# Moving five of seventeen first 3x3 convolutions of an image to VectorE, and two smaller edits

## The chip, the cores and the metric

The kernel runs on one core of a Trainium2 chip. It has a matrix engine (TensorE, PE in the profile; PEld is its loading of weights), a vector engine (VectorE, DVE), an activation engine (ScalarE, ACT), GpSimd (POOL) and SyncE (SP). Here the last two mostly issue DMA transfers. Results of TensorE land in PSUM, an accumulator memory, and another engine must copy them out ("evict" them). The metric is the device time of one execution in microseconds.

## The reference, cut to what matters

The input `x` is 8 images of 32 channels, 128 x 128, float32. All is float32 unless said. `CK = 32 * 8 = 256`.

```python
# layer 0, on g = group_norm(x)
# for each pixel: SSD over 3x3 patches with the 25 shifts of a 5x5 window, the 8 nearest,
# and those 8 shifted copies of g as 256 channels
xb = patch_match_stack(g)
dct = conv1x1(xb, dct_w, groups=C)
h = relu(conv3x3_depthwise(conv1x1(xb, w1), w2))       # "first" pair of convolutions
h = relu(conv3x3_depthwise(conv1x1(h, w3), w4))        # second
wiener = sigmoid(conv3x3_depthwise(conv1x1(h, w5), w6))  # third
x = x + conv1x1(conv1x1(wiener * dct, inv_dct_w, groups=C), agg_w)
# layer 1
x = x + conv5x5(group_norm(x), kernel, padding=2)
```

## The kernel before, in words

**Steps and slots.** Each image is worked in bands of R = 8 rows. There are 17 steps for an image (n = 0 to 16; the last, n = NS = 16, has no new rows and finishes those that the 3x3 convolutions still owe), and 136 for all eight, in one unbroken loop over s (line 917). Each step has four slots, i = 3, 2, 1, 0 in this order (line 928). Slot 1 does the first pair of convolutions (w1, w2) on the band of step s. Slot 2 does the second pair on the band of one step earlier, slot 3 the third on that of two steps earlier, and slot 0 the final part of that band: the product with the grouped 1x1 `dct_w` (`final_dct`, line 749), and in the next slot the sum over channels (`final_add`, line 762).

**Two halves of the channels.** The 256 channels are split. The upper 128 are always convolved by VectorE: `pointwise_v` (line 627) makes the 1x1 convolution with 128 x 128 products into the padded tile tv, ScalarE starts the accumulator (line 685), and VectorE adds the eight other taps with one instruction each (line 688). The lower 128 are convolved by TensorE: `pointwise_t` (line 647) makes the 1x1 convolution with 128 x 32 products into a tile t that has four row phases on the partitions, two transfers on SP (lines 670, 672) build the shifted copies, and `depthwise_t` (line 696) multiplies with small matrices of taps (line 709), which ScalarE evicts with the nonlinearity (line 721). `rows_before_t` and `rows_before_v` carry the two rows above a band over to the next step.

**The order of the work.** On TensorE, VectorE and ScalarE the program's order is the queue's order (ORDERED, line 15). SP and GpSimd are ordered by a planner. The loop writes the order out by hand with generators: a slot's TensorE convolution (dt) is issued in the next slot, in slot 0 ahead of the gather and elsewhere behind it; the last activation of VectorE's convolution (dv) comes at the end of the next slot.

**The gather.** While one band is convolved, the next is gathered: four units of work a step, one in each slot. `gather_load` (line 548) has GpSimd load a broadcast of indices into ib, five buffers; `gather_select` (line 578) makes ScalarE turn each ib into a 0/1 matrix sel with two instructions (lines 584, 585), for two halves, so four instructions a unit; `gather_pixels` (line 588) multiplies these with the shifted pixels on TensorE and has ScalarE evict them to xb (line 606). In slot order the load is three units ahead, the selection one, and both stand in the loop before `tick` and `pointwise_t`.

**Tasks.** The block matching of the next image, the normalisation and the 5x5 convolution of layer 1 are generators in queues D (VectorE), A (ScalarE), P and Q (TensorE). Each VectorE task has a cost in credits; `total` (line 883) is 183.8 for an image, and `tick` (line 886) lets tasks run as the credit owed grows: an image's total is spread over 14 steps (10 for the first image), two fifths of a step's share in slot 0 and a fifth in each other slot, and at most 6 credits stay owed.

Of the kernel before, what the change touches and what calls it, by code (L numbers as in the profile page):

```python
# [13 lines left out]
ALU = mybir.AluOpType  # L14
# [10 lines left out]
QW = TW + 4  # L25
HR = 38
HX = W + 4
SR = 6
EPS = 1e-5

# [13 lines left out]
def bm3d_conv_preact(  # L44
# [72 lines left out]
    tv = [const.tile([P, R + 2, W + 2], F32, name=f"tv{i}") for i in range(3)]  # L117
    for t in tv:
        nc.gpsimd.memset(t, 0.0)
    dwv = const.tile([P, 3, 9], F32, name="dwv")  # L120
    for n, w in enumerate((w2, w4, w6)):
        nc.sync.dma_start(dwv[:, n], w[P:CK].rearrange("p o a b -> p (o a b)"))
# [152 lines left out]
    def mixes():  # L275

        dq = work.tile([P, 2, K], F32, name="dq", tag="dq", bufs=1)
        for k in range(K):
            for m in range(2):
                nc.sync.dma_start(  # L280
                    dq[16 * k : 16 * (k + 1), m],
                    dct_w.rearrange("(m c i) k a b -> k m c (i a b)", m=2, i=K)[k, m],
                )
        m16 = work.tile([P, 16], F32, name="m16", tag="m16", bufs=1)
        yield "D", 1.0
        nc.vector.tensor_add(
            m16, cst[:, C_M32 : C_M32 + 16], cst[:, C_M32 + 16 : C_M32 + C]
        )
# [12 lines left out]
        for m in range(2):  # L301
            yield "D", 0.5
            ib = work.tile([P, P], F32, name=f"ib_{m}", tag="xm")
# [67 lines left out]
    def sources(b, xn):  # L371


        xl = dram.tile([H, W, C], F32, name=f"xl_{b}", tag="xl")
        for r in range(0, 32, 4):
            yield "P", 0
            pt = ps_x.tile([P, 4, P], F32, name=f"px_{b}_{r}", tag="x")
            for q in range(4):
                nc.tensor.transpose(pt[:, q], xn[:, 3 + r + q, 2 : 2 + W], ident)
            xs = work.tile([P, 4, P], F32, name=f"xs_{b}_{r}", tag="ct")  # L380
            nc.scalar.copy(xs, pt)
            for q in range(4):
# [68 lines left out]
    def costs(b, i, sq, idx):  # L451
# [35 lines left out]
        for h in range(0, R, 4):  # L487
# [6 lines left out]
            ct = work.tile([P, 4, P], F32, name=f"ct_{b}_{i}_{h}", tag="ct")  # L494
# [13 lines left out]
    def places(b, idx, i):  # L508
# [5 lines left out]
        o = work.tile([P, 256], F32, name=f"o_{b}_{i}", tag="lin_o", bufs=1)  # L514
        ct = work.tile([P, 256], F32, name=f"cn_{b}_{i}", tag="lin_c", bufs=1)
# [96 lines left out]
    def rows_before_t(i, b, n):  # L612

        t = tb[i - 1]
        if n < NS:
            nc.sync.dma_start(t[0:64, :, 0], t[64:P, :, 3])
        else:
            nc.gpsimd.memset(t[0:64, :, 0], 0.0)
# [8 lines left out]
    def pointwise_v(i, b, n, lhsT, src):  # L627
# [5 lines left out]
        for h in range(0, r1, 4):  # L633
# [10 lines left out]
            a = max(h, r0)  # L644
            nc.scalar.copy(v[:, 2 + a : 2 + h + hr, 1 : 1 + W], ps[:, a - h : hr])  # L645

    def pointwise_t(i, b, n, lhsT, src):
        t = tb[i - 1]
        nb = 2 if n < NS else 1
        if n == NS and i == 1:  # L650
            nc.gpsimd.memset(t[:, :, 2], 0.0)
        else:
            for q in range(2):
                ps = ps_x.tile([P, 2, 2, W], F32, name=f"p{i}_{b}_{n}_{q}", tag="x")
                for e in range(2):
                    s = slice(C * (2 * q + e), C * (2 * q + e + 1))
                    for g in range(2):
                        rows = src(g)
                        for r in range(4):
                            nc.tensor.matmul(  # L660
                                ps[C * r : C * (r + 1), e, :nb],
                                lhsT[:, g, s],
                                rows[:, r : r + 4 * nb - 3 : 4],
                                start=g == 0,
                                stop=g == 1,
                            )
                nc.scalar.copy(t[:, 2 * q : 2 * q + 2, 2 : 2 + nb], ps[:, :, :nb])  # L667
            for r in range(i - 1) if n == 0 else range(i - 1, 4) if n == NS else ():
                nc.gpsimd.memset(t[C * r : C * (r + 1), :, 2], 0.0)
        nc.sync.dma_start(t[64:P, :, 0:nb], t[0:64, :, 2 : 2 + nb])  # L670
# [2 lines left out]

    def depthwise_v(i, b, n):
        v = tv[i - 1]
        nr = R if n < NS else 4
        out_ = accp.tile([P, R, W], F32, name=f"acc{i}_{b}_{n}_1", tag=f"acc{i}1")
        acc = out_[:, :nr]
        for k, (dy, dx) in enumerate(
# [16 lines left out]
    def depthwise_t(i, b, n):  # L696
# [4 lines left out]
            ps_dw.tile([P, 2, 2, W], F32, name=f"pw{i}_{b}_{n}_{u}", tag=f"dw{u}")  # L701
            for u in range(2)
        ]
        for u in range(2):
            hi = 96 if u == 0 else P
            for dx in (0, -1, 1):
                xa, xz = max(0, -dx), min(W, W - dx)
                for j in range(4):
                    nc.tensor.matmul(  # L709
                        pt[u][C * j : C * (j + 1), :, :nb, xa:xz],  # L710
                        dwd[0:hi, i - 1, u, j, dx + 1],
                        t[0:hi, j, :, :nb, xa + dx : xz + dx],
                        start=dx == 0,
                        stop=True,
                        skip_group_check=True,
# [2 lines left out]
        acc = accp.tile([P, R, W], F32, name=f"acc{i}_{b}_{n}_0", tag=f"acc{i}0")  # L718
        rows = acc.rearrange("p (k e) w -> p e k w", e=4)
        for u in range(2):  # L720
            nc.scalar.activation(rows[:, u:4:2, :nb], pt[u][:, :, :nb], funcs[i - 1])  # L721
        rows_before_t(i, b, n)
        accs[i, b, n][0] = acc

# [64 lines left out]
    def layer1(b):  # L789
# [22 lines left out]
                nc.gpsimd.dma_start(xys[c], x1d[b][c : c + 4].rearrange("c y x -> y c x"))  # L812

        def normalise(c):
            xm = work.tile([P, 4, W], F32, name=f"xm_{b}_{c}", tag="xm")
            for i in range(4):
                nc.vector.tensor_scalar(
                    xm[:, i],
# [67 lines left out]
    def tick(b, i):  # L886

        now[0] += 1
        owed[0] += total / (NS - 2 if b else NS - 6) * (0.4 if i == 0 else 0.2)
        owed[0] -= run("D", owed[0]) if owed[0] > 0 else 0  # L890
        owed[0] = min(owed[0], 6.0)

# [8 lines left out]
    with tc.manual_schedule(engines=ORDERED):  # L901
# [8 lines left out]
            unit(gather_pixels, u - 3)  # L910
        u = 4

        dt = dv = kept = iter(())

        later = lambda: None

        for s in range(len(steps) + 2):
# [10 lines left out]
            for i in (3, 2, 1, 0):  # L928
# [6 lines left out]
                if live and i:  # L935
                    src = source(i, bi, ni)
                    pointwise_v(i, bi, ni, lws[i - 1], src)
                    new_v, new_t = depthwise_v(i, bi, ni), depthwise_t(i, bi, ni)
                    accs[i, bi, ni] = [None, next(new_v)]
                later()  # L940
                later = lambda: None
# [8 lines left out]

                run("Q")
                if s < len(steps):
                    unit(gather_select, u + 1)
                    unit(gather_load, u + 3)
                    tick(b, i)
                next(new_v, None)
                if live and i:
                    pointwise_t(i, bi, ni, lws[i - 1], src)
                next(kept, None)
                if not i:  # L960
                    next(dt, None)
# [78 lines left out]
```

## Time and profile before

| what | value |
|---|---|
| median of three runs | 7131.84 us (7118.07 to 7140.6) |
| the profiled execution | 7131.18 us, span 7129.4 us |
| mean granted TensorE clock | 0.978 |
| TensorE busy | 6700.9 us, 94% |
| VectorE busy | 5840.1 us, 82% |
| ScalarE busy | 5061.7 us, 71% |
| GpSimd busy | 2738.3 us, 38% |
| VectorE, taps of the upper half (line 688) | 3264 instructions, 4084.0 us, mean 1253 ns |
| TensorE, 3x3 of the lower half (line 709) | 19584 instructions, 2179.5 us |
| ScalarE, selections (lines 584 and 585) | 2048 instructions, 2249.8 us |

The profile is of one execution. "Busy" is the time in which an engine executes instructions; matmuls overlap each other, so the mean of one times the count is more than the busy time of their group. A row of the waits reads "engine, tile and line that waited <- what ended the wait: us in all, times, longest". A row of the timeline reads "start, length, engine, line, operation, out<-in, shapes, count", with the idle time just before it in brackets. The granted clock is the share of full speed that TensorE was allowed to run at.

### The profile page before, as it was taken

The numbers are of one execution on the slowest core, as the hardware profiler recorded it, in microseconds if no ns is written. First come the engines' busy times: TensorE is split into PE (matmuls) and PEld (weight loads), VectorE is DVE, ScalarE is ACT, GpSimd is POOL, SyncE is SP. The second block draws the span as 40 slices with busy tenths as digits, with TensorE's granted clock in tenths as the row PEclk, the third lists the DMA queues.
The fourth block names the chain that finished last, engine by engine and source line by source line (L and its number), as shares of the span: only waits on it lengthen the run. The fifth ranks groups of instructions, "written<-read, shape, count | busy, mean of one in ns | idle before, by whom it ended". The sixth has DMA issues, their size and how long they took to land. (4 is left out here: it accounts for less than half of the span.)

```text
span 7129.4 us, 229485 instructions
## 1 busy us (share of the span) xinstructions
PE 6700.9 (94%) x100226; PEld 3166.8 (44%) x100226; DVE 5840.1 (82%) x8606; ACT 5061.7 (71%) x6706; POOL 2738.3 (38%) x4599
## 2 busy tenths in 40 slices
PE   4699999999999999999999999999999999999997
PEld 1344444444444444444444444444444444444443
DVE  6689978888888898878888898888978889767675
ACT  4687768677686777867677776877768677666762
POOL 6244336333353343533335343543335333232222
PEclk8899999999999999999999999999999999999999
DMA  3566756666565575666656666566656666555652
GB/s 81 130 145 151 155 129 153 142 148 149 134 156 143 138 166 125 160 145 145 154 127 160 141 152 140 142 161 150 152 130 150 151 145 147 125 146 139 149 134 63
DMA packets 765484, 1007.70 MB, mean 141 GB/s; under 512 B 215008, under 2 KB 578592, under 8 KB 764480
## 3 DMA queue, kind: packets, MB, share of 16 engines
q0 software_dynamic: 378400, 733.67, 42.5%
q1 hardware_dynamic: 381056, 256.86, 17.0%
q8 instruction: 788, 12.91, 0.8%
q10 hardware_dynamic: 5024, 2.49, 0.2%
q14 instruction: 216, 1.77, 0.1%
HBM read 542.24 MB, written 217.01 MB: 106 GB/s over the span
## 5 line engine op out<-in xcount | busy, mean ns | idle before, releaser
L688 DVE SCALAR_TENSOR_TENSOR acc<-tv,dwv,acc 128x1024 f32<-128x1024 f32 (+1 forms) x3264 | 4084.0, 1253 | 223.1 <-ACT acc L685 109.5
L709 PE MATMUL pw<-t,dwd 128*32 128x508 f32 (+6 forms) x19584 | 2179.5, 592 | 156.8 <-DMA t<-t 109.4
L709 PEld LDWEIGHTS pw<-t,dwd 128*32 128x32 f32 (+1 forms) x19584 | 702.3, 111 | 1393.8 <-issue 1205.9
L570 POOL DMA_DIRECT2D ib<-idxd x1024 | 575.2, 563 | 1881.5 <-ACT sel L585 1764.8
L584 ACT ACTIVATE ib<-ib,nplace 128x1024 bf16<-128x1024 bf16 x1024 | 1165.4, 1138 | 25.6 <-DMA ib<-idxd 25.6
L585 ACT ACTIVATE sel<-ib 128x1024 f32<-128x1024 bf16 x1024 | 1084.4, 1059 | 32.6
L660 PE MATMUL p<-acc,lw 128*32 128x256 f32 x17408 | 994.1, 375 | 10.3 <-issue 10.0
L637 PE MATMUL pv<-acc,lw 128*128 128x512 f32 (+1 forms) x2112 | 971.9, 602 | 10.5 <-DVE acc L760 6.3
L606 ACT COPY xb<-pg 128x512 f32<-128x512 f32 x512 | 303.6, 593 | 713.5 <-PE pg L599 713.1
L645 ACT COPY tv<-pv 128x512 f32<-128x512 f32 (+2 forms) x784 | 444.8, 584 | 482.0 <-PE pv L637 463.6
L660 PEld LDWEIGHTS p<-acc,lw 128*32 128x32 f32 x17408 | 562.8, 110 | 429.6 <-issue 81.0
L721 ACT ACTIVATE acc<-pw 128x512 f32<-128x512 f32 (+1 forms) x816 | 452.8, 584 | 341.2 <-PE pw L709 340.8
L599 PEld LDWEIGHTS pg<-sel,xt 128*32 128x32 f32 x45056 | 591.2, 111 | 225.7 <-issue 126.1
L599 PE MATMUL pg<-sel,xt 128*32 128x48 f32 x45056 | 593.6, 206 | 82.9 <-issue 53.1
L780 DVE TENSOR_TENSOR xr<-xr,pa 128x256 f32<-128x256 f32 (+2 forms) x136 | 55.1, 405 | 717.9 <-PE pa L773 698.8
L637 PEld LDWEIGHTS pv<-acc,lw 128*128 128x128 f32 x2112 | 381.0, 191 | 407.7 <-issue 376.7
L410 DVE TENSOR_TENSOR df<-xn 128x786 f32<-128x786 f32 (+2 forms) x576 | 529.0, 969 | 17.2 <-PE pd L425 14.6
L667 ACT COPY t<-p 128x512 f32<-128x512 f32 x800 | 423.0, 570 | 119.8 <-PE p L660 116.5
L418 ACT ACTIVATE df<-df 128x786 f32<-128x786 f32 (+2 forms) x576 | 461.1, 862 | 50.4 <-DVE df L410 49.3
L685 ACT ACTIVATE acc<-tv,dwv 128x1024 f32<-128x1024 f32 (+1 forms) x408 | 459.8, 1127 | 45.8 <-PE pa L773 32.1
L637 PE MATMUL pv<-xb,lw 128*128 128x512 f32 x1024 | 475.7, 607 | 0.0
L757 PE MATMUL pc<-xf,ldct 128*128 128x512 f32 (+2 forms) x1056 | 470.9, 588 | 0.0
(128 smaller groups left out, 6397.3 us busy)
## 6 DMA issues: line engine op xcount, KB each, us to landing
ib<-idxd POOLq DMA_DIRECT2D x1024, 256.0 KB
xbd<-xb POOLq DMA_DIRECT2D x128, 1024.0 KB
xf<-xbd POOLq DMA_DIRECT2D x480, 256.0 KB
t<-t SPq DMA_DIRECT2D x792, 128.0 KB, 4.8
t<-t SPq DMA_DIRECT2D x384, 256.0 KB, 4.9
tv<-tv SPq DMA_DIRECT2D x384, 130.0 KB, 4.1
xt<-xtd POOLq DMA_DIRECT2D x240, 176.0 KB
xl<-xs POOLq DMA_DIRECT2D x256, 64.0 KB
```

What stands on the lines that cost most here:

```text
L410: nc.vector.tensor_sub(df[:, :, ca:cz], xn[:, r0 : r0 + SR, ca:cz], xn[:, r0 + dy : r0 + dy + SR, ca + dx : cz + dx],)
L418: nc.scalar.activation(df[:, :, ca:cz], df[:, :, ca:cz], AF.Square)
L570: nc.gpsimd.dma_start(ib.rearrange("p k y x -> p (k y x)"), idxd[b][s4 // 8, s4 % 8, 4 * k0 : 4 * k0 + 8] .rearrange("k x -> (k x)") .part ...
L584: nc.scalar.activation(ib, ib, AF.Square, bias=nplace)
L585: nc.scalar.activation(sel, ib, AF.Relu, scale=-1.0, bias=1.0)
L599: nc.tensor.matmul(pg[C * j : C * (j + 1), :, xa:xz], xt[:, t], sels[j // 2][:, j % 2, :, xa:xz], start=True, stop=True,)
L637: nc.tensor.matmul(ps[:, :hr], lhsT[:, g, P:CK], src(g)[:, h : h + hr], start=g == 0, stop=g == 1,)
L660: nc.tensor.matmul(ps[C * r : C * (r + 1), e, :nb], lhsT[:, g, s], rows[:, r : r + 4 * nb - 3 : 4], start=g == 0, stop=g == 1,)
L685: nc.scalar.activation(acc, rows, AF.Copy, scale=tap)
L688: nc.vector.scalar_tensor_tensor(acc, rows, tap, acc, op0=ALU.mult, op1=ALU.add)
L709: nc.tensor.matmul(pt[u][C * j : C * (j + 1), :, :nb, xa:xz], dwd[0:hi, i - 1, u, j, dx + 1], t[0:hi, j, :, :nb, xa + dx : xz + dx], start ...
L757: nc.tensor.matmul(ps[:, : z - a], ldct[:, m], xf[:, m, a:z], start=True, stop=True)
```

## The change

Three edits come together.

1. In steps n = 3, 5, 8, 10 and 13 of each image (DENSE), the first pair's lower 128 channels are convolved as the upper ones are. `pointwise_w` makes the 1x1 convolution with 128 x 128 products into a new padded tile tw, and `depthwise_w` has ScalarE start the accumulator, VectorE add eight taps, and ScalarE apply the ReLU. The eight taps are issued in slot 0 and the ReLU at the end of slot 3 (`old`). Since t and tw keep their rows in different layouts, eight transfers take two rows from t to tw before such a step (in `rows_before_t`) and eight take two rows from tw back to t in it. Tasks are charged 10.5 credits for each such step, and the image's total is raised by as much.
2. `gather_select` and `gather_load` move behind `gather_pixels` in the loop, so behind the evictions of `pointwise_t` and of the gather on ScalarE.
3. In the last step (n = 16) only the rows that count are made: `depthwise_v` makes i rows in place of 4, `depthwise_t` and `pointwise_t` leave out row phases that nobody reads.

To make room, the tiles xm, ib (of the setup), xs and ct share one tag with three buffers (before: two tags with two each), and the tiles o and cn of `places` lie in the buffer of v.

```diff
+DENSE = (3, 5, 8, 10, 13)
...
-            xs = work.tile([P, 4, P], F32, name=f"xs_{b}_{r}", tag="ct")
+            xs = work.tile([P, 4, P], F32, name=f"xs_{b}_{r}", tag="ct", bufs=3)
...
-        if n < NS:
+        if i == 1 and n + 1 in DENSE:
+            for q in range(4):
+                for r in range(2):
+                    nc.sync.dma_start(
+                        tw[C * q : C * (q + 1), r, 1 : 1 + W],
+                        t[C * (2 + r) : C * (3 + r), q, 3],
+                    )
+        elif n < NS:
             nc.sync.dma_start(t[0:64, :, 0], t[64:P, :, 3])
...
+    def pointwise_w(lhsT, src):
+
+        for h in range(0, R, 4):
+            ps = ps_x.tile([P, 4, W], F32, name=f"pvw_{h}", tag="x")
+            for g in range(2):
+                nc.tensor.matmul(
+                    ps, lhsT[:, g, 0:P], src(g)[:, h : h + 4], start=g == 0, stop=g == 1
+                )
+            nc.scalar.copy(tw[:, 2 + h : 6 + h, 1 : 1 + W], ps)
+        for q in range(4):
+            for r in range(2):
+                nc.sync.dma_start(
+                    tb[0][C * r : C * (r + 1), q, 0],
+                    tw[C * q : C * (q + 1), R + r, 1 : 1 + W],
+                )
+
+    def depthwise_w(b, n):
+        acc = accp.tile([P, R, W], F32, name=f"acc1_{b}_{n}_0", tag="acc10")
+        nc.scalar.activation(acc, tw[:, 1 : 1 + R, 1 : 1 + W], AF.Copy, scale=dww[:, 4:5])
+        yield
+        for k in (0, 1, 2, 3, 5, 6, 7, 8):
+            nc.vector.scalar_tensor_tensor(
+                acc,
+                tw[:, k // 3 : k // 3 + R, k % 3 : k % 3 + W],
+                dww[:, k : k + 1],
+                acc,
+                op0=ALU.mult,
+                op1=ALU.add,
+            )
+        yield
+        yield
+        nc.scalar.activation(acc, acc, funcs[0])
+        accs[1, b, n][0] = acc
...
+        nr = 4 if n < NS else i - 1
...
-                        for r in range(4):
+                        for r in range(nr):
...
-        nr = R if n < NS else 4
+        nr = R if n < NS else i
...
+        nh = [2 if n < NS else (i + 1 - u) // 2 for u in range(2)]
...
-                for j in range(4):
+                for j in range(4 if nh[u] else 0):
...
-        owed[0] += total / (NS - 2 if b else NS - 6) * (0.4 if i == 0 else 0.2)
+        owed[0] += (total + 10.5 * len(DENSE)) / (NS - 2 if b else NS - 6) * (0.4 if i == 0 else 0.2)
...
-                    new_v, new_t = depthwise_v(i, bi, ni), depthwise_t(i, bi, ni)
+                    dense = i == 1 and ni in DENSE
+                    new_v = depthwise_v(i, bi, ni)
+                    new_t = depthwise_w(bi, ni) if dense else depthwise_t(i, bi, ni)
...
-                    unit(gather_select, u + 1)
-                    unit(gather_load, u + 3)
                     tick(b, i)
                 next(new_v, None)
-                if live and i:
+                if live and i and dense:
+                    pointwise_w(lws[0], src)
+                    next(new_t)
+                    owed[0] -= 10.5
+                elif live and i:
                     pointwise_t(i, bi, ni, lws[i - 1], src)
                 next(kept, None)
                 if not i:
                     next(dt, None)
                 if s < len(steps):
                     unit(gather_pixels, u)
+                    unit(gather_select, u + 1)
+                    unit(gather_load, u + 3)
                     u += 1
                 if i:
                     next(dt, None)
                 run("A")
                 next(dv, None)
+                next(old, None)
                 next(dt, None)
-                kept, dv, dt = dv, new_v, new_t
+                kept, old, dv, dt = dv, dt, new_v, new_t
```

More of the change, by code (lines that the diff above doesn't have):

```diff
@@ L119, in bm3d_conv_preact @@
         nc.gpsimd.memset(t, 0.0)
+    tw = const.tile([P, R + 2, W + 2], F32, name="tw")
+    nc.gpsimd.memset(tw, 0.0)
+    dww = const.tile([P, 9], F32, name="dww")
+    nc.sync.dma_start(dww, w2[0:P].rearrange("p o a b -> p (o a b)"))
     dwv = const.tile([P, 3, 9], F32, name="dwv")
@@ L302, in mixes @@
             yield "D", 0.5
-            ib = work.tile([P, P], F32, name=f"ib_{m}", tag="xm")
+            ib = work.tile([P, P], F32, name=f"ib_{m}", tag="ct", bufs=3)
             nc.vector.tensor_tensor(
@@ L493, in costs @@
                 held.clear()
-            ct = work.tile([P, 4, P], F32, name=f"ct_{b}_{i}_{h}", tag="ct")
+            ct = work.tile([P, 4, P], F32, name=f"ct_{b}_{i}_{h}", tag="ct", bufs=3)
             nc.scalar.copy(ct[:, :, 0 : 4 * NO], pt[:, :, 0 : 4 * NO])
@@ L513, in places @@
         yield "D", 2.6
-        o = work.tile([P, 256], F32, name=f"o_{b}_{i}", tag="lin_o", bufs=1)
-        ct = work.tile([P, 256], F32, name=f"cn_{b}_{i}", tag="lin_c", bufs=1)
+        oc = work.tile([P, R, W + 2], F32, name=f"oc_{b}_{i}", tag="v", bufs=1)
+        oc = oc.rearrange("p r w -> p (r w)")
+        o, ct = oc[:, 0:256], oc[:, 256:512]
         nc.vector.tensor_copy(
@@ L666, in pointwise_t @@
                             )
-                nc.scalar.copy(t[:, 2 * q : 2 * q + 2, 2 : 2 + nb], ps[:, :, :nb])
+                nc.scalar.copy(
+                    t[: C * nr, 2 * q : 2 * q + 2, 2 : 2 + nb], ps[: C * nr, :, :nb]
+                )
             for r in range(i - 1) if n == 0 else range(i - 1, 4) if n == NS else ():
@@ L707, in depthwise_t @@
                 xa, xz = max(0, -dx), min(W, W - dx)
-                for j in range(4):
+                for j in range(4 if nh[u] else 0):
                     nc.tensor.matmul(
-                        pt[u][C * j : C * (j + 1), :, :nb, xa:xz],
+                        pt[u][C * j : C * (j + 1), : nh[u], :nb, xa:xz],
                         dwd[0:hi, i - 1, u, j, dx + 1],
-                        t[0:hi, j, :, :nb, xa + dx : xz + dx],
+                        t[0:hi, j, : nh[u], :nb, xa + dx : xz + dx],
                         start=dx == 0,
@@ L720, in depthwise_t @@
         for u in range(2):
-            nc.scalar.activation(rows[:, u:4:2, :nb], pt[u][:, :, :nb], funcs[i - 1])
+            if nh[u]:
+                nc.scalar.activation(
+                    rows[:, u : u + 2 * nh[u] - 1 : 2, :nb], pt[u][:, : nh[u], :nb], funcs[i - 1]
+                )
         rows_before_t(i, b, n)
@@ L814, in normalise @@
         def normalise(c):
-            xm = work.tile([P, 4, W], F32, name=f"xm_{b}_{c}", tag="xm")
+            xm = work.tile([P, 4, W], F32, name=f"xm_{b}_{c}", tag="ct", bufs=3)
             for i in range(4):
@@ L911, in bm3d_conv_preact @@
         u = 4
-        dt = dv = kept = iter(())
+        dt = dv = kept = old = iter(())
         later = lambda: None
```

## The prediction, made before the changed kernel was run

> **What bounds the kernel now.** I read the page's busy times first, then the windows of one image step by step, then the waits, then the order of time around one wait.
>
> ```profile
> PE 6700.9 (94%) x100226; PEld 3166.8 (44%) x100226; DVE 5840.1 (82%) x8606; ACT 5061.7 (71%) x6706; POOL 2738.3 (38%) x4599
> ```
>
> TensorE looks like the bound, with VectorE at 82%. An average hides the stages, so I cut image 4 into groups of steps. A window runs from the final product (line 757) of one step to that of the next. The columns are length, then the busy time of PE, PEld, DVE, ACT, POOL, clock, DMA.
>
> ```profile
> 3836.90:4059.00 222.10, 220.20 (x3098) 102.50 (x3095) 182.44 (x285) 157.18 (x202) 71.77 (x123) 1.00 0.63 145
> 4059.00:4352.80 293.80, 286.66 (x4509) 135.75 (x4508) 264.23 (x503) 218.79 (x290) 111.58 (x195) 0.99 0.67 154
> 4352.80:4483.80 131.00, 125.95 (x1787) 56.57 (x1785) 105.30 (x96) 83.34 (x109) 37.98 (x70) 1.00 0.55 128
> 4483.80:4683.10 199.30, 190.74 (x3144) 97.68 (x3140) 172.82 (x188) 169.14 (x235) 119.68 (x185) 0.99 0.64 156
> 6646.80:6879.80 233.00, 229.18 (x3685) 108.22 (x3681) 169.99 (x151) 172.69 (x220) 66.66 (x122) 1.00 0.64 148
> ```
>
> They are steps 3 to 6, 7 to 12, 13 to 15, then 16 with 0 to 2 of the next image; the last is five steps of the last image. TensorE has 2 us of idle time in steps 3 to 6 and VectorE 40. In steps 7 to 12 VectorE is busy 264 of 294 us, so only 30 us are left there. The last image has no block matching for a next one, and VectorE has 63 us left in five steps.
>
> ```profile
> PE pw L709 <- DMA t<-t: 109.4, 53, 12.1
> POOL ib L570 <- ACT sel L585: 1764.8, 468, 13.0
> ACT ib L584 <- DMA ib<-idxd: 25.6, 6, 10.0
> ...
> 3611.21 1.13 ACT L584 ACTIVATE ib<-ib,nplace 128x1024 bf16<-128x1024 bf16 x1
> 3612.38 1.06 ACT L585 ACTIVATE sel<-ib 128x1024 f32<-128x1024 bf16 x1
> 3613.34 1.05 ACT L667 COPY t<-p 128x512 f32<-128x512 f32 x2
> 3614.42 0.59 SPq L670 DMA_DIRECT2D t<-t  x1
> 3615.06 1.14 SPq L672 DMA_DIRECT2D t<-t  x1
> 3620.24 7.03 PE L709 MATMUL pw<-t,dwd 96*32 96x512 f32 x48 [2.30 <-DMA t<-t]
> ```
>
> The first line is TensorE's largest wait with a named cause; the last six show how it comes about. The product whose result t holds had ended at 3610.96, but ScalarE was in its four selection instructions and copied t out only at 3613.34. Its two transfers landed late, the convolution waited 2.30 us, and then took 7.03 us, where an undisturbed one takes 5.33.
>
> **The change, part by part.** All sums are against the profiled execution, 7131.2 us (span 7129.4 and 1.8 around it), which is 0.7 below the median: no correction.
>
> *Selections behind the evictions.* Nothing is added. From the first window (334 us) to the last image's end the trace has 48 waits for t<-t of together 88 us, and 18 of the products behind them are slow, together by 36 us (14 of them by 1.70 each). So at most 124 us can go. About two fifths of the waits lie in steps where VectorE has only 2 to 4 us of idle time (0, 9 to 12), which will bind next; I take 70. From the other side: between slot 0 and slot 3 the selections now stand ahead of the copies to tv. At 6659.26 ScalarE started such a copy; four selection instructions (1.138 + 1.059, twice) would put it some 3 to 4 us later and VectorE's convolution with it. What hides that is VectorE's tasks ahead of it, or its idle time (40 us in steps 3 to 6); with no cover in any step it would cost 3.5 x 136 = 476 us. I take 0. GpSimd's two loads a slot (0.56 us each) move with the selections, so their lead over the reader stays two slots; on its queue they now stand behind the store of xb, which waits 77 us in all for its eviction. ScalarE waits 25.6 us for the loads; twice that would cost 26 more. I take 0.
>
> The Trainium skill, "TensorE: Matmul & The Clock Gate", section "HAM oscillation", asks only that TensorE have no idle gap above about 3.4 us. The trace disagrees: 2.30 us was enough for the half rate, while at 5663.8 a gap of 1.57 left 5.33. By the rule the 36 us would not be there to win, and this part would be worth 50.
>
> *The convolution moved.* Per dense step (40 of them) TensorE loses 48 passes of line 709, 5.33 us, and 64 of line 660 (3.66) for 8 like line 637 (3.70): 213 us in all. VectorE gains 8 x 1.284 = 10.3 us, 411 in all. ScalarE gains line 685 and 692 (1.15 + 1.06) and loses two of line 721 (0.60 each): 1.0 us each, 41 in all, hidden at 71% busy. SP issues 8 transfers before the step and 8 in it, and four fewer of the old: 12 x 0.59 = 7.1 us per dense step. They read or fill rows that are used a step (50 us) later against 4.8 to land, so I take 0; should the planner put eight ahead of a t<-t transfer that is just in time, that convolution starts 4.7 us later, 40 x (4.7 + 1.7) = 256 us at the worst. The tiles that now share three buffers (xs, ct, xm) can make ScalarE wait for VectorE's searches; bounded by the present 62.6 us that VectorE waits for ct, taken as 0.
>
> What matters is when the new result is wanted. It is made in slot 0 and read by the first product of slot 2. From the end of line 757, TensorE has 1.09 (gather) + 1.07 (line 773) + 3.70 + 3.66 + 1.09 = 10.6 us of other work. VectorE needs 0.69 + 10.3 and ScalarE 1.06: 12.1, plus VectorE's backlog b. So TensorE will wait 1.5 + b. Behind the waiting activation on ScalarE stand only slot 2's evictions, since the next selections and the gather's eviction are ahead of it. The 5.33 saved is used up at b = 3.8, or at 2.1 if the wait halves the clock. The backlog can be read from when the four multiplications end against line 757's end. In step 5 VectorE stood waiting, in step 13 it was far behind:
>
> ```profile
> 3950.47 0.69 DVE L760 TENSOR_TENSOR acc<-acc,pc 128x512 f32<-128x512 f32 x1 [3.41 <-PE pc L757]
> 4352.35 10.52 DVE L688 SCALAR_TENSOR_TENSOR acc<-tv,dwv,acc 128x1024 f32<-128x1024 f32 x8
> 4362.78 2.48 DVE L760 TENSOR_TENSOR acc<-acc,pc 128x512 f32<-128x512 f32 x4
> ```
>
> In image 4, b is about 0.2 in step 3, 0 in 5, 2.8 in 8, 4.5 in 10, 8.1 in 13, and 1.4 in the last image. The gains are 3.6 and 3.8 in steps 3 and 5; steps 8, 10 and 13 come to +0.7, +2.4 and +6.0 lost. The 10.5 credits taken off hold tasks back in slots 0 and 3 and shrink these losses; I take 0, 1 and 3. That leaves 3.4 per image, 24 for seven, and 5 x (5.33 - 2.9) = 12 for the last: 36 us.
>
> *The pace of tasks.* Tasks go from 13.1 to 16.9 credits a step, less 10.5 in a dense one, so they still end with step 13. A credit is 0.90 us (5840 less 4084 in line 688, 322 in 760 and 105 in 780 and 781, over eight images: 166 us for 183.8). Steps without the extra work get 3.4 us more; steps 7, 9, 11 and 12 had 6.8, 3.9, 1.7 and 8.1 us of VectorE idle. I take a loss of 1.5 per image, 10 us.
>
> *The last step.* A convolution takes 48 passes in 2.79 us (0.058 each). At half the width a pass takes 0.030 (line 660: 64 in 1.95), so the three keep 24 x 0.030, 48 x 0.030 and 24 of each: 2.1 + 1.3 + 0.7 less, 32 us over eight images. VectorE's 24 instructions shrink from 0.751 to about 0.35, 0.43 and 0.59 (line 329 with 128 elements, line 522 with 256, and between for 384): 57 us, where it already idles 8 to 12 a step. I take 25.
>
> Sum: 7131 - 70 - 36 + 10 - 25 = **7010**.
>
> [...]
>
> **The rivals.**
>
> *TensorE stays the bound everywhere.* For it: it idles 2 us in steps 3 to 6, and the totals after would still be 6701 - 213 - 32 = 6456 against 5840 + 411 - 57 = 6194. Against: steps 7 to 12. All of it but the 1.5 us waits: 7131 - 213 + 60 - 32 - 124 = 6822.
>
> *VectorE becomes the bound: slower.* Place: the wait in slot 2. In steps 7 to 12 an undense window needs 34.4 + 15.2 = 49.6 us of VectorE against some 46.5 of TensorE. If that surplus is never drained, b is 2 in steps 3 and 5 and about 6, 8 and 11 in 8, 10 and 13; with the half clock these cost 3.9 + 5.9 + 8.9, less 3.6: 15 per image, 106 for seven. Selections then bring 30, the last step 25: 7182; with 3 us in each of four undense windows too, 7266. It decides above a mean b of 3.8; the five of image 4 have 3.1. For it: step 13's 8.1. Against: steps 3 and 5, and the credits.
>
> *The parts cancel.* The waits for t<-t turn into waits for a late tv, and the dense steps bring nothing: 7131 - 25 = 7106.
>
> **How the numbers follow.** A measurement of this kernel can tell about 0.3% (21 us) from no change; its runs span 7118 to 7141. Chances: my forecast 0.45 (6930 to 7085), TensorE the bound 0.17 (6790 to 6930), cancelling 0.14 (7085 to 7150), VectorE the bound 0.24 (7150 to 7270). Faster is the first two and 0.05 of the third, same 0.09, slower 0.24. Cutting about a tenth at each end gives 6850 to 7190.
>
> **What would show it.** Right: waits for t<-t well under half of 109; t copied straight after its product; VectorE near 6190 busy; the first product of slot 2 late by 1 to 3 us in steps 3 and 5 and by more in 8 to 13, behind ScalarE's last activation of the new accumulator; steps 3 to 6 shorter, 7 to 12 not. Wrong: steps 7 to 12 shorter by 10 us or more (b drained), or new waits of TensorE for selections, for transfers queued on SP, or for tv.

## The result: slower by 3.8%

The changed kernel takes 7404.5 us (median of four runs, 7391.9 to 7411.5) against 7136.2 for the kernel before. The ratio is 1.0378, 95% interval 1.0353 to 1.0403. The forecast was 7010, and 6850 to 7190 the range. The profiled execution has a span of 7409.4 us, 280 more than before. The medians and ratios below leave out two executions, of 10554.0 us (the kernel before) and 23234.3 us (the kernel with the third pair), whose granted clocks were 0.605 and 0.553.

The busy times of the changed kernel, from its page:

```profile
PE 6642.3 (90%) x95234; PEld 3105.2 (42%) x95234; DVE 6195.0 (84%) x8926; ACT 5118.6 (69%) x6698; POOL 2732.6 (37%) x4600
```

VectorE is at 6195 us, as worked out (6194), and ScalarE 57 us up (41 worked out). TensorE should have lost 244 us and lost 59: the passes that were taken out are gone (17472 of the 3x3 in place of 19584), and others became slower, with the mean granted clock at 0.954 in place of 0.978. Its idle time went from 428 to 767 us. So the time went into pauses of TensorE and into slow products around them.

The same groups of steps of image 4 (3 to 6, 7 to 12, 13 to 15, 16 with 0 to 2), changed kernel; length first, then busy PE, PEld, DVE, ACT, POOL, then clock, DMA share and GB/s:

```profile
4004.90:4231.80 226.90, 207.84 (x2919) 96.82 (x2915) 202.73 (x293) 154.75 (x196) 69.36 (x120) 0.96 0.55 135
4231.80:4554.90 323.10, 291.25 (x4250) 136.45 (x4246) 282.68 (x509) 226.10 (x294) 114.70 (x199) 0.95 0.61 138
4554.90:4690.00 135.10, 124.04 (x1741) 55.60 (x1737) 113.91 (x105) 84.40 (x109) 36.21 (x67) 0.96 0.51 124
4690.00:4910.60 220.60, 201.73 (x3010) 97.95 (x3007) 174.92 (x208) 174.09 (x241) 119.36 (x187) 0.98 0.60 144
```

All four groups became longer, by 5, 29, 4 and 21 us. In steps 7 to 12 VectorE had 30 us of idle time before and has 40 now, TensorE 7 before and 32 now. Neither is full: they wait.

What TensorE waits for in the changed kernel, from the waits:

```profile
PE pv L651 <- ACT acc L692: 240.1, 40, 8.9
PE pd L431 <- ACT df L424: 140.7, 89, 3.1
PE pi L541 <- DVE oc L532: 67.1, 12, 19.7
...
PE pw L762 <- DMA t<-t: 28.1, 10, 6.0
```

And the row of the squares in the kernel before:

```profile
PE pd L425 <- ACT df L418: 29.5, 29, 2.9
```

Line 651 is the 1x1 product of `pointwise_v`, line 692 the ReLU of the new dense convolution, lines 424 and 431 the squares of the block matching and the product that sums them. Before, the second wait was 29.5 us in 29 times, and the first had no counterpart. The wait for the indices of the block matching (lines 532 and 541) was 42.7 us before. The wait for t<-t, 109.4 us before, is down to 28.1.

The 40 waits for the ReLU are nearly all alike: 38 of them are between 5.89 and 5.97 us, whatever VectorE had to do. One of them, in the order of time, ScalarE and then TensorE and VectorE:

```profile
7034.82 0.59 ACT L613 COPY xb<-pg 128x512 f32<-128x512 f32 x1 [0.91 <-PE pg L606]
7035.30 1.15 ACT L591 ACTIVATE ib<-ib,nplace 128x1024 bf16<-128x1024 bf16 x1
7036.48 1.06 ACT L592 ACTIVATE sel<-ib 128x1024 f32<-128x1024 bf16 x1
7037.45 1.13 ACT L591 ACTIVATE ib<-ib,nplace 128x1024 bf16<-128x1024 bf16 x1
7038.61 1.06 ACT L592 ACTIVATE sel<-ib 128x1024 f32<-128x1024 bf16 x1
7039.58 1.04 ACT L692 ACTIVATE acc<-acc 128x1024 f32<-128x1024 f32 x1
...
7034.02 0.76 PE L606 MATMUL pg<-sel,xt 128*32 128x48 f32 x51 [0.34 <-issue]
7040.67 5.99 PE L651 MATMUL pv<-acc,lw 128*128 128x512 f32 x8 [5.89 <-ACT acc L692]
...
7029.33 7.89 DVE L682 SCALAR_TENSOR_TENSOR acc<-tw,dww,acc 128x1024 f32<-128x1024 f32 x6
7037.14 0.41 DVE L836 TENSOR_TENSOR xr<-xr,pa 128x256 f32<-128x256 f32 x1
```

VectorE's last tap ended at about 7037.1. ScalarE was then in the moved selections, which stand in its queue between the gather's eviction and the ReLU, and came to the ReLU at 7039.58 without having been idle since 7034.8. From the end of the gather to the end of the ReLU it is 0.59 + four selection instructions + 1.04, which is the 5.9. The product behind the pause then took 5.99 us, where it takes 3.70 at full clock; behind the 40 pauses it took between 5.11 and 6.71. Pause and slow product are 8.2 us, and the convolution that was saved is 5.33.

So the theory after the result: two parts of the change get in each other's way on ScalarE, and the moved selections also stand before the squares. The rival is the one of the prediction: VectorE is late with its extra taps.

### The profile page after: what moved, and what is told of

Read it like the earlier page. It is cut to its first block, busy times and chain, and to the rows that moved or that the text cites. A ratio compares the mean times of both kernels' runs of the same rounds, so it can differ in the third digit from the quotient of the medians.

```text
span 7409.4 us, 220482 instructions
## 1 busy us (share of the span) xinstructions
PE 6642.3 (90%) x95234; PEld 3105.2 (42%) x95234; DVE 6195.0 (84%) x8926; ACT 5118.6 (69%) x6698; POOL 2732.6 (37%) x4600
## 5 line engine op out<-in xcount | busy, mean ns | idle before, releaser
L739 DVE SCALAR_TENSOR_TENSOR acc<-tv,dwv,acc 128x1024 f32<-128x1024 f32 (+3 forms) x3264 | 4031.1, 1237 | 294.9 <-ACT acc L736 175.0
L762 PE MATMUL pw<-t,dwd 128*32 128x508 f32 (+6 forms) x17472 | 1923.8, 588 | 96.4 <-issue 43.9
L651 PE MATMUL pv<-acc,lw 128*128 128x512 f32 (+1 forms) x2112 | 1066.2, 651 | 278.2 <-ACT acc L692 240.1
L762 PEld LDWEIGHTS pw<-t,dwd 96*32 96x32 f32 (+1 forms) x17472 | 613.8, 111 | 1178.7 <-issue 1125.2
L709 PE MATMUL p<-acc,lw 128*32 128x256 f32 x16768 | 1027.0, 381 | 9.3 <-issue 5.3
L651 PEld LDWEIGHTS pv<-acc,lw 128*128 128x128 f32 x2112 | 415.6, 209 | 734.5 <-issue 425.6
L716 ACT COPY t<-p 128x512 f32<-128x512 f32 (+1 forms) x720 | 404.7, 578 | 425.3 <-PE p L709 414.1
L431 PE MATMUL pd<-df,neg 128*32 128x390 f32 (+2 forms) x2304 | 372.2, 531 | 146.0 <-ACT df L424 140.7
L775 ACT ACTIVATE acc<-pw 128x512 f32<-128x512 f32 (+1 forms) x728 | 381.2, 567 | 143.6 <-PE pw L762 143.6
L736 ACT ACTIVATE acc<-tv,dwv 128x1024 f32<-128x1024 f32 (+3 forms) x408 | 454.7, 1114 | 28.4 <-PE pa L829 14.9
```

Of the source, the lines that this page charges most:

```text
L651: nc.tensor.matmul(ps[:, :hr], lhsT[:, g, P:CK], src(g)[:, h : h + hr], start=g == 0, stop=g == 1,)
L709: nc.tensor.matmul(ps[C * r : C * (r + 1), e, :nb], lhsT[:, g, s], rows[:, r : r + 4 * nb - 3 : 4], start=g == 0, stop=g == 1,)
L736: nc.scalar.activation(acc, rows, AF.Copy, scale=tap)
L739: nc.vector.scalar_tensor_tensor(acc, rows, tap, acc, op0=ALU.mult, op1=ALU.add)
L762: nc.tensor.matmul(pt[u][C * j : C * (j + 1), : nh[u], :nb, xa:xz], dwd[0:hi, i - 1, u, j, dx + 1], t[0:hi, j, : nh[u], :nb, xa + dx : xz ...
```

## The experiments

Each is given by its edit against the changed kernel, unless another is named. Ratios are against the kernel before on the same chip. Where "..." stands, lines of a diff are left out.

### The ReLU ahead of the selections

```diff
                     unit(gather_pixels, u)
+                next(old, None)
+                if s < len(steps):
                     unit(gather_select, u + 1)
                     unit(gather_load, u + 3)
...
                 next(dv, None)
-                next(old, None)
```

> The changed kernel, with the last activation (ReLU) of the dense convolution issued before the four selection instructions of its slot instead of behind them. Theory A (ScalarE's order): the constant wait of 5.92 us at the first product of slot 2, 40 times, is the gather's eviction (0.59), four selection instructions (4.3) and the ReLU (1.04) behind the gather. Then the wait falls to what VectorE leaves, 3.4 us where its taps end 2.3 us after the gather, less elsewhere, and most of the slow products behind it (5.99 for 3.70) go: 40 x (2.5 to 4.8) = 100 to 190 us less, about 7215 to 7305. Theory B (VectorE's backlog, the prediction's rival): VectorE is what is late; the wait stays near 5.9 and the time near 7405.

Measured: 7289.8 us, ratio 1.0193 (1.0176 to 1.0210), by the ratios 1.85%, some 130 us, less than the changed kernel. Its waits:

```profile
PE pv L651 <- ACT acc L692: 110.5, 40, 5.3
PE pd L431 <- ACT df L424: 132.7, 87, 3.1
```

And, from the view of the ReLU's line, what ScalarE sat idle for before it (us, times); in the changed kernel this list is empty:

```profile
  DVE acc L682: 41.8, 21
```

The wait more than halved. Nineteen of the 40 are at 1.63 to 1.67 us, which is the gather's eviction and the ReLU alone; in the others ScalarE now does wait for VectorE. Both theories hold a part: the order was what bound, VectorE is next.

### Half of the taps

Four of the eight taps of the dense convolution are left out, so that result is incomplete.

```diff
-        for k in (0, 1, 2, 3, 5, 6, 7, 8):
+        for k in (0, 1, 2, 3):
```

> The changed kernel with four of the eight taps of the dense convolution left out (40 x 4 VectorE instructions, 206 us of VectorE; that result is not computed in full). Theory A (ScalarE's order): VectorE was not what TensorE waited for; the 40 waits stay at 5.9 us and the time within 60 us of 7405. Theory B (VectorE's backlog): the waits shrink by 5.1 us each and with them the slow products, 200 to 300 us less: 7100 to 7200.

Measured: 7405.4 us in a single execution, with 199 us less of busy VectorE.

```profile
PE pv L651 <- ACT acc L692: 240.0, 40, 8.9
```

The waits are what they were with all eight taps (240.1). Theory A holds, and the rival falls for the kernel as it was changed.

### Half of the taps, with the ReLU ahead

The same edit on the kernel with the ReLU ahead of the selections; again the result is incomplete.

> The kernel with the ReLU ahead of the selections (7290), with four of the eight taps of the dense convolution left out (206 us of VectorE; that result is not computed in full). Theory A: with the order mended VectorE is now late in half of the 40 waits (those above 1.65 us), so all 40 fall to 1.65, which is the gather's eviction and the ReLU, and the time falls by 40 to 110 us: 7180 to 7250. Rival: what is left of the loss has nothing to do with the taps but with the selections ahead of the squares; the waits above 1.65 stay or the time stays within 30 us of 7290.

Measured: 7202.8 us, ratio 1.0055 (1.0038 to 1.0072), by the ratios 1.4%, some 100 us, less than with all eight taps.

```profile
PE pv L651 <- ACT acc L692: 66.5, 40, 1.7
PE pd L431 <- ACT df L424: 139.5, 88, 3.1
```

All 40 waits are now 1.7 us or less. So with the order mended, VectorE's lateness is worth some 100 us; with the order as in the change it is worth nothing, since it was covered.

### The selections alone

The kernel before, with only the selections moved:

```diff
-                    unit(gather_select, u + 1)
-                    unit(gather_load, u + 3)
                     tick(b, i)
...
                     unit(gather_pixels, u)
+                    unit(gather_select, u + 1)
+                    unit(gather_load, u + 3)
```

> The kernel before with the selections and loads moved behind the gather and nothing else. Theory A (squares): the squares of the block matching now stand behind 4.3 us of selections on ScalarE, and TensorE's product of squares waits for them as in the changed kernel (118 us in all, against 8 before, and slow products behind); the waits for t<-t (109) go. Net 20 to 120 us slower: 7155 to 7255. Rival (the prediction): only the waits for t<-t go, 70 us faster, about 7065.

Measured: 7230.4 us, ratio 1.0115 (1.0098 to 1.0132).

```profile
PE pd L425 <- ACT df L418: 144.7, 104, 3.2
PE pw L709 <- DMA t<-t: 28.5, 19, 5.2
```

The waits for t<-t went from 109 to 28 us, as forecast. The wait for squares came, 115 us more than before, and the product of squares itself took longer (252.8 us of TensorE before, 299.1 now, each instruction counted up to the start of the next). Less 81, plus 115, plus 46 makes 80, near the 82 between the medians. The list is not complete: the two profiled executions differ by 92 us, the wait for the indices (line 534) rose from 42.7 to 72.1, and pauses before the gather for which the profile names no cause fell from 53.1 to 23.7. One place where squares are waited for, ScalarE and then TensorE:

```profile
2059.69 0.59 ACT L606 COPY xb<-pg 128x512 f32<-128x512 f32 x1 [5.49 <-PE pg L599]
...
2064.45 3.08 ACT L418 ACTIVATE df<-df 128x780 f32<-128x780 f32 x4
...
2065.34 2.76 PE L425 MATMUL pd<-df,neg 128*32 128x390 f32 x14 [1.11 <-ACT df L418]
```

ScalarE waited 5.49 us for the gather with no selection to do, then had the four selections before it, and the squares came 4.2 us after the eviction. TensorE waited 1.11 us for the first square and then went at ScalarE's pace, which made four squares in 3.08 us. The granted clock is 1.00 in this stretch and 0.980 in the whole run, so here TensorE is fed slowly and its clock is not cut. Where the selections stood before, they filled that idle time.

VectorE, too, waits more: for the accumulator that ScalarE starts from tv. The kernel before, then this one:

```profile
DVE acc L688 <- ACT acc L685: 109.5, 97, 5.8
...
DVE acc L688 <- ACT acc L685: 288.8, 132, 8.6
```

How much of these 179 us reaches the end no run shows.

### The selections back

The changed kernel with the selections where they were; dense steps, pace and last step stay.

> The changed kernel with the selections and loads back where they were before the change; the dense steps, the pace and the last step stay. Theory A (ScalarE's order): the wait for the ReLU is no longer 5.92; it is 1.5 us plus VectorE's backlog, 1.5 to 5, the waits for t<-t come back, those for squares go: 7060 to 7150. Theory B (VectorE's backlog): the dense steps alone cost the time, 7250 or more.

Measured: 7215.8 us, ratio 1.0094 (1.0077 to 1.0111). So the dense steps, with their pace and the last step's edit, are a loss of about 68 us of their own.

```profile
PE pv L651 <- ACT acc L692: 144.5, 40, 6.7
PE pd L431 <- ACT df L424: 35.3, 32, 2.9
```

Again what ScalarE sat idle for before the ReLU:

```profile
  DVE acc L682: 1.9, 4
```

The waits for squares are back at their old size. The wait for the ReLU is 3.6 us in the mean, and ScalarE waited for VectorE directly before it only 4 times, 1.9 us: its own queue is behind here too. In 31 of the 40 it came to the ReLU from four selections, two copies of t and the gather's eviction without a pause between them. TensorE also waits 54.7 us for VectorE's multiplications of slot 0 (line 816), 6.3 before. The granted clock is still low, 0.958. The time lies between the two forecasts.

### The pace of tasks

On the kernel of the last paragraph, credits as before the change:

```diff
-        owed[0] += (total + 10.5 * len(DENSE)) / (NS - 2 if b else NS - 6) * (0.4 if i == 0 else 0.2)
+        owed[0] += total / (NS - 2 if b else NS - 6) * (0.4 if i == 0 else 0.2)
...
-                    owed[0] -= 10.5
```

> The kernel with the dense steps, the last step and the selections where they were (7216), with the tasks' pace of the kernel before: no credits added and none charged. Theory A (the prediction's small term): the pace matters by 10 to 40 us, since charged tasks keep VectorE free in slots 0 and 3; without it the 40 waits grow (mean 3.6 now, 4 to 7 then): 7220 to 7300. Rival: the faster pace of the undense steps is itself a cost, and the time falls to 7150 to 7190.

Measured: 7312.7 us, ratio 1.0219 (1.0195 to 1.0242), about 1.25% slower than with the charge. The wait for the ReLU is 211.5 us, up to 9.8 each. Charging the dense steps is worth some 90 us. ScalarE sat idle for VectorE directly before the ReLU for only 17 us, in 7 of the 40 waits. In 19 others, 119.5 of the 211.5 us, it sat idle one place earlier: for the differences of the block matching (line 416), which VectorE makes behind its taps, and whose squares (line 424) `run("A")` puts ahead of the ReLU. One of these, ScalarE, VectorE and TensorE:

```profile
4070.44 0.58 ACT L613 COPY xb<-pg 128x512 f32<-128x512 f32 x1 [0.33 <-PE pg L606]
4073.12 1.74 ACT L424 ACTIVATE df<-df 128x786 f32<-128x786 f32 x2 [2.09 <-DVE df L416]
4074.76 1.04 ACT L692 ACTIVATE acc<-acc 128x1024 f32<-128x1024 f32 x1
...
4060.88 10.53 DVE L682 SCALAR_TENSOR_TENSOR acc<-tw,dww,acc 128x1024 f32<-128x1024 f32 x8
...
4072.12 1.84 DVE L416 TENSOR_TENSOR df<-xn 128x786 f32<-128x786 f32 x2
...
4075.85 6.23 PE L651 MATMUL pv<-acc,lw 128*128 128x512 f32 x8 [5.48 <-ACT acc L692]
```

The charge keeps these tasks out of the slot; with it (the run before) such a chain through line 424 occurs once in 40.

### The last step alone

The kernel before with the last step's edit (nr, nh) and nothing else.

> The kernel before with the last step's edit alone. The prediction has 25 us less for it (32 of TensorE, 57 of VectorE, where VectorE already idles): 7105 to 7125. Rival: these steps are bound by something else (the order of slots, transfers), and the time stays within 10 us of the kernel before.

Measured: 7150.6 us, ratio 1.0001 (0.9988 to 1.0014). Its convolutions shrank from 2.79 us each to 0.86, 1.51 and 2.15, 31 us in all, as worked out. But TensorE's busy time is 6698.4 against 6700.9: the full-size passes of the 3x3, by shape, rose from 774.8 + 742.5 + 421.8 + 420.3 = 2359.4 to 2380.6 us, and the granted clock was 0.972. It is 0.972 to 0.975 in all twelve executions, and 0.975 to 0.980 in the 28 of the kernel before beside them. Why the clock fell is not settled; the gain did not reach the end.

### Where no squares wait, and squares first

Two other places for the selections, both on the kernel with the last step's edit. In the first they go behind the gather only in slots in which ScalarE has no task; in the second they stay behind the gather and the tasks go ahead of them.

```diff
-                    unit(gather_select, u + 1)
-                    unit(gather_load, u + 3)
                     tick(b, i)
+                early = bool(queues["A"])
+                if s < len(steps) and early:
+                    unit(gather_select, u + 1)
+                    unit(gather_load, u + 3)
...
                     unit(gather_pixels, u)
+                    if not early:
+                        unit(gather_select, u + 1)
+                        unit(gather_load, u + 3)
```

> The last step's edit, and selections and loads behind the gather only in slots in which no task waits for ScalarE (so no squares of the block matching); in the other slots they stay where they were before. Theory A (squares): TensorE's wait for squares stays as in the kernel before, waits for t<-t go in the slots that were moved; 20 to 60 us less than with the last step's edit alone: 7050 to 7100. Rival: the waits for t<-t were covered anyway, and nothing is gained beyond the last step's edit.

Measured: 7139.9 us, ratio 0.9985 (0.9971 to 0.9999): a gain of about 0.15%, below the forecast. The waits for t<-t only fell to 91.8 us in 40 times, from 113.7 in 48 with the last step's edit alone. In 24 of the 40, 56.7 us, the selections still stand on ScalarE directly ahead of the copy of t. The wait for the indices rose from 41.7 to 71.4 us.

```diff
-                    unit(gather_select, u + 1)
-                    unit(gather_load, u + 3)
                     tick(b, i)
...
                     unit(gather_pixels, u)
+                run("A")
+                if s < len(steps):
+                    unit(gather_select, u + 1)
+                    unit(gather_load, u + 3)
...
-                run("A")
```

> The last step's edit, and in all slots the order gather's eviction, squares, selections on ScalarE. Theory A (squares): the waits for squares (122 us and 46 us of slow products in the kernel with the selections alone moved) go; the selections come up to 3.4 us later, and between slots 0 and 3 the next gather may wait 0 to 3 us for them in some 15 steps of an image's block matching: 7040 to 7140. Rival: what TensorE waited for was not the squares' place but ScalarE's total work; the time stays near 7210.

Measured: 7178.5 us, ratio 1.0041 (1.0026 to 1.0056).

```profile
PE pg L599 <- ACT sel L585: 49.5, 31, 10.8
PE pw L714 <- ACT acc L727: 35.3, 23, 3.2
PE pg L599 <- ACT tv L645: 31.8, 29, 2.3
PE pw L714 <- DMA t<-t: 29.9, 21, 3.8
PE pd L425 <- ACT df L418: 27.7, 26, 2.9
```

The waits for t<-t and for squares are both small, as the theory says, and two thirds of the loss of the moved selections are gone. In their place TensorE waits for selections and for evictions (lines 727 and 645), so here what was moved back on ScalarE is waited for in its turn. The largest wait of all is that for the indices, 81.6 us. The time lies between the forecast and its rival.

### The dense convolution in the third pair

The selections as in the first of these two, and the dense convolution for the third pair (w6, with the tiles of that pair) in its steps 1, 3 and 5.

```diff
-DENSE = (3, 5, 8, 10, 13)
+DENSE = (1, 3, 5)
...
-                    dense = i == 1 and ni in DENSE
+                    dense = i == 3 and ni in DENSE
```

> Like the kernel that picks the place of the selections, with the dense convolution moved from the first pair to the third, in its steps 1, 3 and 5 of an image (three in place of five, charged 10.5 credits each). Its result is read in slot 0, two long slots after the one that makes it, against two short ones before. Theory A: the wait that ate the gain came from where the result is read; TensorE saves up to 24 x 5.3 = 128 us, of which 30 to 80 reach the end: 6980 to 7060. Rival (VectorE's backlog): the ten us of taps move VectorE's multiplications of slot 0 and the first product of slot 3 instead, and nothing is gained over the kernel without dense steps, or up to 60 us lost.

Measured: 7236.6 us (three executions), ratio 1.0112 (1.0079 to 1.0146): a loss, more than the rival of the expectation gave.

```profile
PE pw L762 <- DMA t<-t: 117.3, 50, 8.1
PE pw L762 <- ACT acc L775: 54.4, 22, 8.1
PE pg L606 <- DVE acc L816: 47.8, 17, 4.1
```

And what ScalarE sat idle for before the last activation of the dense convolution (us, times):

```profile
  DVE acc L682: 81.9, 17
```

Here the gather waits for VectorE's multiplications of slot 0 (line 816), which were pushed back, and the next convolution for an eviction behind a waiting ScalarE. The longer way to the reader did not help.

### Both orders mended, five dense steps and two

The ReLU ahead of the selections, and these behind the gather only in slots without tasks; first with all five dense steps, then with `DENSE = (3, 5)`.

> All five dense steps, the ReLU ahead of the selections, and the selections behind the gather only in slots without tasks for ScalarE. Theory A: both faults of the order are mended, what is left is VectorE's lateness and the half clock behind short pauses: near the kernel before, 7130 to 7190. Rival: the dense steps pay once the order is right: 7000 to 7100.

Measured: 7188.8 us, ratio 1.0048 (1.0032 to 1.0063), at the upper end of theory A.

> As the run with five dense steps and both orders mended, with only steps 3 and 5 dense (tasks charged for two). These are the steps in which VectorE had 40 us idle in four. Theory A: here VectorE is not late, waits are 1.65 to 3 us against 5.33 saved, 16 x 2 to 3.5 us: 30 to 60 us less than the kernel before, 7085 to 7120. Rival: the pauses cost the half clock and the neighbouring steps take the gain back: within 20 us of the kernel before, or slower.

Measured: 7135.8 us, ratio 0.9974 (0.9960 to 0.9989).

```profile
PE pw L762 <- DMA t<-t: 72.0, 34, 4.7
PE pv L651 <- ACT acc L692: 37.2, 16, 4.6
```

This is the fastest kernel of the study, 0.26% under the kernel before and, by the ratios, 3.9% under the changed one. The sixteen waits are 2.3 us in the mean, against 5.33 saved. It is not told apart from the kernel that only places the selections (0.9985); their intervals overlap. By the ratio it is some 19 us under the kernel before, which is what the rival of the expectation gave. With steps 8, 10 and 13 dense as well it is 0.74% slower.

### The sum of the parts

By the ratios: the selections alone 1.15%; dense steps, pace and last step with the selections in their old place 0.94%; the last step alone, which is part of that, 0.01%. Together 2.09 of the 3.78%. The missing 1.7% is what the parts do to each other, and moving the ReLU ahead of the selections takes 1.85% away. Within the intervals the two agree. The kernel with the ReLU ahead still waits 110.5 us for it, so this does not show that nothing else is at work.

## Why the prediction was wrong, point by point

**What bounds the kernel.** Right as far as it went: TensorE, with VectorE next in steps 7 to 12.

**Selections behind the evictions: 70 us less forecast, 82 more measured.** The forecast read the wait for t<-t rightly, and it went (109.4 to 28.5). It counted as readers of ScalarE's queue the gather, tv and VectorE's convolution. It left out the squares, which `run("A")` issues behind the gather and TensorE sums in the next slot; the selections now stand before them, and the wait for squares went from 29.5 to 144.7 us. That is the first failed step: of a moved instruction, what comes behind it in the new place was not gone through to the end. The bound from above (476 us, taken as 0) was for tv. VectorE's wait behind tv did grow by 179 us, and how much of that reaches the end is open. Of the waits that the 70 us start from, the trace has 51 with 94 us in the stretch named, not 48 with 88, which changes little.

**The convolution moved: 36 us less forecast.** With the pace and the last step it makes 51 less; with the selections in their old place it measured 68 more. The work was sized rightly (VectorE 6195 us; the 213 us of TensorE are 212 by their own terms). The wait was put at 1.5 + b by VectorE's chain, 12.1 us against 10.6. The prediction even said that the next selections and the gather's eviction stand ahead of the ReLU on ScalarE, and then counted 1.06 us for ScalarE. ScalarE's own chain behind the gather is 0.59 + 4.3 + 1.04 = 5.9 us, the longer of the two; the wait is the maximum of both, not the one that was worked out. That is the second failed step, and it is where the two edits meet: with the selections in their old place the wait is 3.6 us in the mean. With half of the taps the wait was the same 5.92, and with the ReLU ahead it fell to 1.65 and VectorE's share. With that order the formula is near: 1.65 as the least, and up to 5.3 where VectorE is behind.

**The half clock.** The forecast had 1.7 us for it in each loss of steps 8, 10 and 13, which it then took as 0, 1 and 3, and no other loss by it in the sum. In the run all 40 pauses were followed by a slow product, 2.2 us too long in the mean. The granted clock is 0.951 to 0.963 in the kernels with five full dense steps, 0.956 with half of the taps in the order of the change and 0.970 with the ReLU ahead, 0.965 and 0.968 with three and two dense steps, and 0.972 to 0.980 in those without any. Of the 244 us that TensorE should have lost, 185 came back in longer products. The clock is not all of it: the product of squares takes 301.3 us in place of 252.8, counted as above, though with the selections alone moved it takes 299.1 at a granted clock of 0.980.

**The pace: about 90 us gained by the charge.** The prediction had two terms for it: 10 us lost to faster tasks in the other steps, and the losses of steps 8, 10 and 13 shrunk from 0.7, 2.4 and 6.0 us to 0, 1 and 3, which is 5.1 for an image and 36 for seven. So 26 us gained in all: the right sign and a third of the size. Keeping tasks out of slots 0 and 3 holds the wait for the ReLU down, mostly by keeping squares from standing ahead of it.

**The last step: 25 us forecast, nothing measured** (1.0001), though the 31 us of passes went.

**The rivals.** "VectorE becomes the bound" had the right sign and the right place (the wait in slot 2), with 0.24, but its price (7182 to 7266) is 138 us short, and in the changed kernel its cause is not the one that binds: with half of the taps the waits were the same. "The parts cancel" named the late tv, which came; what it cost is open. The forecast that steps 3 to 6 would be shorter failed as well; they are 5 us longer.

## What to carry to other kernels

When an instruction is moved back in an in-order queue, list everything behind its new place with its reader, not only what it used to delay; a queue that fills an engine's idle time before a late input is doing useful work there. A new wait is the longest of all chains that lead to it, so add up each engine's queue from the same starting point. And work taken off the busiest engine pays only if the engine then stays fed: here the best kernel has two such steps of seventeen, is 0.26% faster than the one before, and cannot be told from one without any.

## What the runs showed of the hardware that was not expected

Taking 31 us of passes off TensorE left its busy time where it was (6700.9 and 6698.4 us); 21 us came back in the remaining passes of the same shapes, at a granted clock of 0.972 in place of 0.978. Behind pauses of 5.9 us and more the same 1x1 product took 5.11 to 6.71 us in 40 of 40 cases; behind pauses of 1.7 us and less (half of the taps, the ReLU ahead) it took 3.70 in 32 of 40. In the whole run the granted clock fell from 0.978 to 0.954 while TensorE's idle share rose from 6 to 10%. Idle time alone does not set it: with the selections alone moved TensorE was idle for 460 us at a clock of 0.980, with the last step alone for 458 us at 0.972. So a saving on TensorE that opens pauses must be charged for the products behind them.
